# The first scan layer's near part: the product of B with dt·u moved from VectorE to GpSimd, B fetched by DMA

## The chip, the cores and the metric

The kernel runs on one core of a Trainium2 chip. Its time is the device time of one execution in microseconds (us). A core has five engines that work side by side, each through its own queue in order: PE (TensorE, matrix products into PSUM, with a second track PEld for loading weights), DVE (VectorE), ACT (ScalarE), POOL (GpSimd) and SP (SyncE, which here issues almost all DMAs). They wait for each other through semaphores. SBUF is the working memory of 128 partitions; PSUM is the small accumulation memory that TensorE writes.

## The reference

Two layers, each `x = x + layer(groupnorm(x))` on a 64 x 64 image with 96 channels. A layer projects to 192 channels and a gate, applies a depthwise 3 x 3 convolution and silu, runs a selective scan in four directions with 16 states per channel, normalises, gates and projects back. The part that the change touches is the scan of the first layer:

```python
def _ssm_scan(u, x_proj_w, dt_proj_w, dt_proj_b, A_log, D_skip):
    x_dbl = u @ x_proj_w
    dt = x_dbl[..., :DT_RANK]
    B_mat = x_dbl[..., DT_RANK:DT_RANK + D_STATE]
    C_mat = x_dbl[..., DT_RANK + D_STATE:]
    dt = jax.nn.softplus(dt @ dt_proj_w + dt_proj_b)
    A = -jnp.exp(A_log)
    log_dA = jnp.einsum('bld,dn->bldn', dt, A)
    dB_u = jnp.einsum('bld,bln->bldn', dt, B_mat) * u[..., None]
    decay = jnp.exp(jnp.cumsum(log_dA, axis=1))
    h = decay * jnp.cumsum(dB_u / (decay + 1e-12), axis=1)
    y = jnp.einsum('bldn,bln->bld', h, C_mat)
    return y + u * D_skip
...
y1 = scan(s1)
y2 = scan(s1[:, ::-1])[:, ::-1]
y3 = scan(s3)
y4 = scan(s3[:, ::-1])[:, ::-1]
```

`s1` is the image by rows, `s3` by columns. Because of the 1e-12, a state's contribution is damped by decay / (decay + 1e-12), so that it is gone some way into the sequence.

## The kernel before

The layers run one after the other (the code's `l` is 0 for the first). Each has a head (projection, convolution, gate), its scans and a tail (normalisation, gate, projection). The second layer's scans take most of the time, from about 260 to 1440 us, and are not touched.

**The near part.** For the first layer, `near_scans` computes only the first 192 tokens (`NEAR`) of each of the four directions, and of most states less: `kinds` has three entries (n tokens, first and last pair of states): (192, 0, 1), (64, 1, 2) and (32, 2, 8). At the end a flag says whether all that was left out is truly gone; a branch (`tc.If`, line 1729) then skips `far_scans`, and all engines load the flag, branch and meet behind it. The 128 partitions of a tile are two states times 64 channels; T counts three blocks of 64 channels.

**Its parts, in order.** `nu` (three PSUM tiles, one for each T) gathers the tokens of the four directions by matrix products, copied to `nus`; `npj` projects them; the result, with the rows of dt, B and C, is copied to `nxd`. C's rows are stored to DRAM (`nC`) and fetched back, each row spread over 64 partitions (`ncb`, six DMAs). B is spread over partitions on TensorE instead: 18 products `nB<-nxd,picked` into a four-bank PSUM tile, with `picked` a table of ones and zeros that GpSimd writes once. `decays` computes the rates `am`. Softplus gives `nv` on ACT and DVE. `steps_of(T)` makes dt and dt·u (`ndt`, `ndu`) and copies each across the halves by DMA, `sums_of(T)` does so for the running sum of dt (`nS`).

**The units.** There are six: (T0, long), (T0, short), (T1, long), (T1, short), (T2, short), (T2, long), where long is the 192-token kind (768 elements a partition) and short the other two together (256 + 768). Unit j needs, by name: `operands(j)` (ACT: `nna` = exp(rate x dt); GpSimd: a memset of its first columns), `weights_of(j)` (ACT: `nnwt`, a tanh of the sums), and then `scan(j)`, all on DVE but the last: the product `nb<-nB,ndu` (one instruction for a long unit, two for a short one), the product with the weight `nb<-nnwt,nb` (scalar_tensor_tensor, STT below), the scan `nnh<-nna,nb`, and the product with C, `nnhc<-nnh,ncb`, on GpSimd (on DVE for the last unit). `nb` lies in PSUM, so DVE makes it there. `add(j)` sums over states on TensorE into `ny`, whose one PSUM buffer serves one T after the other; `sum_up(T)` adds that to `y` on DVE. The tiles `nna`, `nnwt`, `nnh` and `nnhc` have two buffers each.

**The order.** Engines with `Ordered` around them (line 271, so most instructions here show as L271) keep the order in which the program issues them; what is issued without it (`nc.vector`, `nc.sync`) is placed by the scheduler. In the middle, `look_ahead` issues the second layer's weights, some thirty small DMAs, on SP. GpSimd also scales the six halves of `y` by D (`later`, `y<-u,ds`) early in the near part. Behind the branch, the tail begins with loads of `szt` and `xT` on SP.

Of the kernel before, what the change touches and what calls it, by code (L numbers as in the profile page):

```python
# [21 lines left out]
NS = 16  # L22
# [22 lines left out]
def two_ss2d_layers(  # L45
# [231 lines left out]
    def near_scans(weights, later):  # L277
# [5 lines left out]
        with ExitStack() as sc:  # L283
# [5 lines left out]
            def parts(t):  # L289

                return t.rearrange("p (d w) -> p d w", w=NEAR)
# [8 lines left out]
            top = once.tile([128, len(kinds), 3, 4], F32, name="top")  # L300
            most = once.tile([128, len(kinds) + 1, 3], F32, name="most")
            flag = once.tile([1, 1], mybir.dt.int32, name="flag")
            picked = once.tile([32, NP, 128], F32, name="picked")
            nc.gpsimd.tensor_copy(
                picked.rearrange("p m (h w) -> p m h w", h=2),
                i3[0:32, 0:NS].rearrange("p (m h) -> p m h", h=2)
                .unsqueeze(3)
                .to_broadcast([32, NP, 2, 64]),
            )
            for start in later:  # L310
                start()


            us = once.tile([128, 3, 2, 2 * NEAR], F32, name="nus")
            k = NEAR // HW
            pj = pps.tile([128, 2, 512], F32, tag="m", name="npj")[0:NC, :, 0 : 2 * NEAR]
            for T in range(3):
                ps = pps.tile(
                    [128, 4 if T == 2 else 2, 512], F32, tag="yBB"[T], name=f"nu{T}"
                )[:, 0:2]  # L320
                pe.matmul(
                    ps[:, 0, 0:NEAR], wide[0], u[T][:, 0:NEAR], start=True, stop=True
                )
# [15 lines left out]
                for q, copy in enumerate((act.copy, dve.tensor_copy)):  # L339
                    copy(us[:, T, q], ps[:, q, 0 : 2 * NEAR])  # L340
            for T in range(3):
                for q in range(2):
                    pe.matmul(
                        pj[:, q], xw[HALF[q], 0, T, :], us[HALF[q], T, q],
                        start=(T == 0), stop=(T == 2),
                    )
# [3 lines left out]
            dve.tensor_copy(xq[:, 1], pj[:, 1])  # L350


            C = []
            for w, m0, m1 in kinds:
                rows = dram.tile([NS, 4 * w], F32, name=f"nC{w}")
                sp.dma_start(
                    out=rows.rearrange("n (d w) -> n d w", w=w),
                    in_=parts(xd[NC - NS : NC])[:, :, 0:w],
                )
                C.append(rows)  # L360


            pd = []
            for T in range(3):
# [60 lines left out]
            def reach():  # L425
                for i, (n, m0, m1) in enumerate(kinds):
                    dve.tensor_mul(
                        top[:, i],
                        S.rearrange("p t q (d w) -> p t (q d) w", w=NEAR)[:, :, :, n - 1],
                        most[:, i, :].unsqueeze(2).to_broadcast([128, 3, 4]),  # L430
                    )
                dve.reduce_max(
                    most[:, len(kinds), 0:1], top.rearrange("p i a b -> p (i a b)"), axis=AX.X
                )

                pe.transpose(Bf[0:1, at : at + 128], most[:, len(kinds), 0:1], ident)

            def reached():
                ps = Bf[0:1, at : at + 128]
                dve.reduce_max(most[0:1, len(kinds), 1:2], ps, axis=AX.X)  # L440
                dve.tensor_scalar(flag, most[0:1, len(kinds), 1:2], GONE, None, ALU.is_le)


            Bp = pps.tile([128, 4, 512], F32, tag="B", name="nB")
            Bf = Bp.rearrange("p a b -> p (a b)")
            B, cb, at = [], [], 0
            for n, m0, m1 in kinds:
                B.append([])
                t = once.tile([128, m1 - m0, 4 * n], F32, name=f"ncb{n}")
                for m in range(m0, m1):  # L450
                    dst = Bf[:, at : at + 4 * n]
                    if n == NEAR:
                        for s in (slice(0, 512), slice(512, WN)):
                            pe.matmul(
                                dst[:, s], picked[:, m, :], xd[0:32, s], start=True, stop=True
                            )
                    else:
                        pe.matmul(
                            dst.rearrange("p (d w) -> p d w", w=n), picked[:, m, :],
                            parts(xd[0:32])[:, :, 0:n], start=True, stop=True,  # L460
                        )
                    at += 4 * n
                for h, half in enumerate(HALF):
                    rows = C[len(cb)][2 * m0 + h : 2 * m1 : 2]
                    sp.dma_start(out=t[half], in_=rows.unsqueeze(0).to_broadcast(t[half].shape))
                B[-1] = Bf[:, at - 4 * n * (m1 - m0) : at]
                cb.append(t.rearrange("p n w -> p (n w)"))


            units = [(T, ks) for T in range(3) for ks in ((0,), (1, 2))]  # L470
# [39 lines left out]
                        AF.Tanh, bias=lneps, scale=am[:, 1, 0, T, m : m + 1],  # L510
                    )

            def scan(j):
                T, ks = units[j]
                a, wt, h, hc = live[j]

                b = pps.tile([128, 2, 512], F32, tag="m", name=f"nb{j}")
                b = b.rearrange("p a w -> p (a w)")
                o = 0
                for i in ks:  # L520
                    n, m0, m1 = kinds[i]
                    k = m1 - m0
                    dve.tensor_mul(
                        b[:, o : o + 4 * n * k].rearrange("p (n d w) -> p n d w", n=k, w=n),
                        B[i].rearrange("p (n d w) -> p n d w", n=k, w=n),
                        four(du, T)[:, :, 0:n].unsqueeze(1).to_broadcast([128, k, 4, n]),
                    )
                    o += 4 * n * k
                b = b[:, 0:o]
                dve.scalar_tensor_tensor(b, wt, 1.0, b, ALU.add, ALU.mult)  # L530
                dve.tensor_tensor_scan(h, a, b, 0.0, ALU.mult, ALU.add)
                o = 0
                for i in ks:
# [46 lines left out]
                    dve.tensor_add(to, of, to)  # L580

            steps_of(0)
            steps_of(1)
            sums_of(0)
            steps_of(2)
            operands(0)
# [6 lines left out]
            for j in range(len(units)):  # L593
                if j > 1:
                    weights_of(j)
                if 0 < j < len(units) - 1:
                    operands(j + 1)
                scan(j)
                if j == 1:
                    reach()  # L600
                if j == 2:
# [1219 lines left out]
```

## Time and profile before

| | us |
|---|---|
| median of 4 runs (1469.22 to 1479.03) | 1474.74 |
| the profiled execution | 1472.07 |
| its span, first to last instruction | 1470.3 |
| near part, first `nu` product to the meeting behind the branch | 73.50 to 148.81 |
| the six scans of units on DVE, first start to last end | 107.16 to 140.17 |
| DVE, nine products `nb<-nB,ndu` in all | 7.1 |
| PE, 18 products `nB<-nxd,picked` | 86.75 to 93.09 |
| POOL, six `y<-u,ds` | 75.92 to 92.88 |

The profile's times count from the start of the span. The timeline lists instructions of each engine in order, equal neighbours merged: start, duration, engine, line, operation, output <- inputs, partitions x elements, count, and in brackets how long the engine had been idle and what ended that. SPq is SP's queue: a row there is a DMA being issued, about 0.6 us each, not its transfer. Over the whole span DVE is busy 91%, POOL 82%, ACT 83%; these are averages over both layers, and say little of the near part.

### The profile page before, as it was taken

What the parts mean: (1) busy time and instruction counts of PE and PEld (TensorE: products, weight loads), DVE (VectorE), ACT (ScalarE), POOL (GpSimd) and SP (SyncE); (2) the same over time, 40 slices, a digit from 0 to 9 for tenths busy, and PEclk for the clock granted to TensorE, in tenths of its full rate; (3) what the DMA queues carried; (4) which work ended last, traced back from release to release, by engine and by line L of the source; (5) the groups of instructions that cost most, each with busy time, mean ns of one, the idle gap of its engine ahead of it and who ended that gap; (6) DMA issues with size and microseconds to landing.
All of it is one profiled execution on the core that took longest, in us unless ns stands there. A gap on an engine that the chain in (4) does not pass through costs nothing.

```text
span 1470.3 us, 17235 instructions
## 1 busy us (share of the span) xinstructions
PE 1209.5 (82%) x5011; PEld 469.6 (32%) x5011; DVE 1338.4 (91%) x925; ACT 1218.2 (83%) x2506; POOL 1212.6 (82%) x667
## 2 busy tenths in 40 slices
PE   5845869788888898988888889888879888887897
PEld 2233323233333332333333333333333233322333
DVE  5967677789999999999999999999998999999996
ACT  5764438699898989999999999999897989897874
POOL 2752039588989898989898989898989898989894
PEclk7965979599999899999999989999998999999999
DMA  3231622626262626262626262626262626262634
GB/s 108 82 96 23 148 54 89 131 58 145 58 145 60 143 60 143 60 144 60 144 59 144 60 145 59 150 61 147 61 143 55 148 62 141 72 144 67 136 104 111
DMA packets 85556, 147.70 MB, mean 100 GB/s; under 512 B 33436, under 2 KB 36700, under 8 KB 85356
## 3 DMA queue, kind: packets, MB, share of 16 engines
q1 hardware_dynamic: 83772, 143.96, 41.3%
q0 software_dynamic: 576, 1.57, 0.5%
q8 instruction: 41, 0.67, 0.2%
q10 hardware_dynamic: 1104, 0.98, 0.2%
q14 instruction: 63, 0.52, 0.1%
HBM read 80.85 MB, written 12.13 MB: 63 GB/s over the span
## 4 chain that ended last, share of the span: by engine, by line
DVE 26%; issue 20%; PE 13%; ACT 13%; POOL 8%; DMA 6%; SPq 3%; DVEq 0%; POOLq 0%; ACTq 0%
DVE h L751 17%; DVE b L751 7%; POOL hc L751 5%; ACT a L751 4%; DMA cb<-C 4%; SPq L751 3%; PE pj L751 3%; ACT bT L751 3%; PE ys L751 3%; PE b L751 2%; DMA xT<-xs 1%; POOL sp L751 1%; POOL ln L751 1%; DMA dt<-sp 1%; PE cp L271 1%
## 5 line engine op out<-in xcount | busy, mean ns | idle before, releaser
L751 POOL TENSOR_TENSOR hc<-h,cb 128x1024 f32<-128x1024 f32 x384 | 902.6, 2370 | 94.7 <-DVE h L751 37.9
L751 DVE TENSOR_TENSOR_SCAN h<-a,carry,b 128x1024 f32<-128x1024 f32 x288 | 664.9, 2338 | 24.0 <-PE b L751 2.8
L751 ACT ACTIVATE a<-dt,am 128x1024 f32<-128x1024 f32 x384 | 439.2, 1144 | 57.6 <-DVE h L751 54.5
L751 PE MATMUL ys<-hc,fold 128*64 128x512 f32 x1536 | 430.6, 640 | 0.0
L751 ACT ACTIVATE bT<-duT,BT 128x192 f32<-128x192 f32 x1012 | 387.9, 447 | 2.9 <-PE b L751 0.8
L751 PE MATMUL b<-ident,bT 128*128 128x128 f32 x1536 | 223.2, 288 | 30.4 <-DVE h L751 19.5
L751 DVE TENSOR_TENSOR b<-b,du 128x1024 f32<-128x1024 f32 x192 | 232.0, 1208 | 8.4 <-PE b L751 8.4
L751 DVE TENSOR_TENSOR_SCAN h<-a,b 128x1024 f32<-128x1024 f32 x96 | 216.4, 2278 | 13.2 <-PE b L751 3.4
L751 PEld LDWEIGHTS b<-ident,bT 128*128 128x128 f32 x1536 | 176.6, 146 | 154.7 <-DVE h L751 92.2
L751 PE MATMUL b<-B,selh 96*128 96x512 bf16 x384 | 117.2, 387 | 125.3 <-DVE h L751 125.1
L751 PEld LDWEIGHTS ys<-hc,fold 128*64 128x64 f32 x1536 | 77.9, 138 | 140.4 <-issue 104.5
L751 PEld LDWEIGHTS <-selh 96*128 96x128 bf16 x384 | 25.7, 98 | 254.1 <-DVE h L751 203.0
L751 PE MATMUL pj<-u,xw 64*124 64x512 f32 x192 | 96.5, 649 | 1.9 <-DVE w L751 1.2
L271 POOL TENSOR_TENSOR tap<-tap,tap 128x512 f32<-128x512 f32 x48 | 61.0, 1275 | 44.3 <-ACT tap L271 42.0
L271 DVE SCALAR_TENSOR_TENSOR acc<-pad,v,acc 128x1052 f32<-128x1052 f32 (+1 forms) x64 | 75.2, 1181 | 2.1
L751 ACT CAST B<-pj 96x512 bf16<-96x512 f32 (+2 forms) x96 | 55.0, 576 | 6.1 <-PE pj L751 6.1
L751 PE MATMUL ys<-y,ident 128*128 128x512 f32 (+1 forms) x120 | 58.9, 592 | 0.0
L751 POOL TENSOR_TENSOR ln<-ln,w 128x512 f32<-128x512 f32 x45 | 57.7, 1283 | 0.0
L751 POOL TENSOR_TENSOR sp<-sp,ln 128x512 f32<-128x512 f32 x45 | 57.6, 1280 | 0.2
L751 POOL TENSOR_TENSOR su<-sp,u 128x512 f32<-128x512 f32 x45 | 57.4, 1276 | 0.0
L751 PE MATMUL pd<-xd,dwb 29*64 29x512 f32 x192 | 54.5, 636 | 0.0
L751 PEld LDWEIGHTS pj<-u,xw 64*124 64x124 f32 x192 | 34.4, 194 | 60.8 <-issue 47.3
(188 smaller groups left out, 1188.0 us busy)
## 6 DMA issues: line engine op xcount, KB each, us to landing
cb<-C SPq DMA_DIRECT2D x256, 256.0 KB
dt<-sp SPq DMA_DIRECT2D x192, 128.0 KB
du<-su SPq DMA_DIRECT2D x180, 128.0 KB
szd<-sz SPq DMA_DIRECT2D x24, 256.0 KB
szt<-szd SPq DMA_DIRECT2D x24, 256.0 KB
xT<-xs SPq DMA_DIRECT2D x8, 384.0 KB
xs<-xT SPq DMA_DIRECT2D x1, 1536.0 KB
xs<-xT SPq DMA_DIRECT2D x8, 192.0 KB
```

The lines of the kernel that those rows point to most:

```text
L271: return lambda *args, **more: tc.keep_in_program_order(op(*args, **more))
L751: return lambda *args, **more: tc.keep_in_program_order(op(*args, **more))
```

## The change

- `picked` and the 18 products that spread B over partitions are gone, and with them the four-bank PSUM tile. The PSUM tiles are dealt out anew: `nu` gets one two-bank buffer for each T (tags y, m, B), `npj` and the test of the flag one of their own (tag j).
- B's rows go the way of C's: two stores to DRAM, six fetches, each row to 64 partitions, now to SBUF. Of B and C alike only the rows of 192 and of 32 tokens are stored; those of 64 are fetched as a cut of the 192. In all, SP issues 16 such DMAs for 9.
- The fetches of C's second and third kind (four DMAs) come after `steps_of(1)`; before, all six stood ahead of `steps_of(0)`.
- The product of B with dt·u is `inputs(j)`, on GpSimd, into an SBUF tile with two buffers; for units 0 and 1 right after `steps_of(0)`, for unit j + 2 after `scan(j)`.
- `scan(j)` begins with the STT, which reads both factors from SBUF and writes PSUM, in two buffers used by turns.

```diff
-            picked = once.tile([32, NP, 128], F32, name="picked")
-            nc.gpsimd.tensor_copy(
...
-            pj = pps.tile([128, 2, 512], F32, tag="m", name="npj")[0:NC, :, 0 : 2 * NEAR]
+            
             for T in range(3):
-                ps = pps.tile(
-                    [128, 4 if T == 2 else 2, 512], F32, tag="yBB"[T], name=f"nu{T}"
-                )[:, 0:2]
+                ps = pps.tile([128, 2, 512], F32, tag="ymB"[T], name=f"nu{T}")
...
+            pj = pps.tile([128, 2, 512], F32, tag="j", name="npj")[0:NC, :, 0 : 2 * NEAR]
...
+            def stored(what, first):
+
+                kept = {}
+                for w in (NEAR, kinds[-1][0]):
+                    rows = dram.tile([NS, 4 * w], F32, name=f"n{what}{w}")
+                    rows = kept[w] = rows.rearrange("n (d w) -> n d w", w=w)
+                    sp.dma_start(out=rows, in_=parts(xd[first : first + NS])[:, :, 0:w])
+                return kept
+
+            def fetched(what, kept, i):
+
+                n, m0, m1 = kinds[i]
+                t = once.tile([128, m1 - m0, 4, n], F32, name=f"n{what}b{n}")
+                for h, half in enumerate(HALF):
+                    if n in kept:
+                        to, of = t[half], kept[n][2 * m0 + h : 2 * m1 : 2]
+                    else:
+                        to, of = t[half, 0], kept[NEAR][2 * m0 + h, :, 0:n]
+                    sp.dma_start(out=to, in_=of.unsqueeze(0).to_broadcast(to.shape))
+                return t.rearrange("p n d w -> p (n d w)")
+
+            rows = stored("B", 0)
+            B = [fetched("B", rows, i) for i in range(len(kinds))]
+            rows = stored("C", NC - NS)
+            cb = [fetched("C", rows, 0)]
...
-            def scan(j):
+            def inputs(j):
                 T, ks = units[j]
-                a, wt, h, hc = live[j]
-
-                b = pps.tile([128, 2, 512], F32, tag="m", name=f"nb{j}")
-                b = b.rearrange("p a w -> p (a w)")
+                b = live["b", j] = nb.tile([128, 1024], F32, tag="nb", name=f"nb{j}")
                 o = 0
                 for i in ks:
                     n, m0, m1 = kinds[i]
                     k = m1 - m0
-                    dve.tensor_mul(
+                    pool.tensor_mul(
                         b[:, o : o + 4 * n * k].rearrange("p (n d w) -> p n d w", n=k, w=n),
                         B[i].rearrange("p (n d w) -> p n d w", n=k, w=n),
                         four(du, T)[:, :, 0:n].unsqueeze(1).to_broadcast([128, k, 4, n]),
                     )
                     o += 4 * n * k
-                b = b[:, 0:o]
-                dve.scalar_tensor_tensor(b, wt, 1.0, b, ALU.add, ALU.mult)
+
+            def scan(j):
+                T, ks = units[j]
+                a, wt, h, hc = live[j]
+                w = a.shape[-1]
+                b = pps.tile([128, 2, 512], F32, tag="mB"[j % 2], name=f"nbw{j}")
+                b = b.rearrange("p a w -> p (a w)")[:, 0:w]
+                dve.scalar_tensor_tensor(b, wt, 1.0, live.pop(("b", j))[:, 0:w], ALU.add, ALU.mult)
                 dve.tensor_tensor_scan(h, a, b, 0.0, ALU.mult, ALU.add)
...
             steps_of(0)
+            inputs(0)
+            inputs(1)
             steps_of(1)
+            cb += [fetched("C", rows, i) for i in range(1, len(kinds))]
             sums_of(0)
...
                 scan(j)
+                if j + 2 < len(units):
+                    inputs(j + 2)
```

More of the change, by code (lines that the diff above doesn't have):

```diff
@@ L302, in near_scans @@
             flag = once.tile([1, 1], mybir.dt.int32, name="flag")
-            picked = once.tile([32, NP, 128], F32, name="picked")
-            nc.gpsimd.tensor_copy(
[L305 to L309, printed above, removed]
             for start in later:
@@ L350, in near_scans @@
             dve.tensor_copy(xq[:, 1], pj[:, 1])
[L353 to L360, printed above, removed]
+            def stored(what, first):
[19 more added lines that the diff above has]
+            cb = [fetched("C", rows, 0)]
             pd = []
@@ L434, in reach @@
                 )
-                pe.transpose(Bf[0:1, at : at + 128], most[:, len(kinds), 0:1], ident)
+                live["most"] = pps.tile([128, 2, 512], F32, tag="j", name="nmost")[0:1, 0, 0:128]
+                pe.transpose(live["most"], most[:, len(kinds), 0:1], ident)
             def reached():
-                ps = Bf[0:1, at : at + 128]
-                dve.reduce_max(most[0:1, len(kinds), 1:2], ps, axis=AX.X)
+                dve.reduce_max(most[0:1, len(kinds), 1:2], live.pop("most"), axis=AX.X)
                 dve.tensor_scalar(flag, most[0:1, len(kinds), 1:2], GONE, None, ALU.is_le)
[L444 to L467, printed above, removed]
             units = [(T, ks) for T in range(3) for ks in ((0,), (1, 2))]
```

## The prediction, made before the changed kernel ran

> **What bounds the kernel now.** I read the windows of the near part first, then its timeline, then the chain of waits behind the branch. The windows (busy us of each engine and instructions in brackets):
>
> ```profile
> core 0: us, PE busy (x) PEld busy (x) DVE busy (x) ACT busy (x) POOL busy (x), PEclk, DMA share, GB/s
> 73.00:97.00 24.00, 18.27 (x82) 12.71 (x78) 13.68 (x20) 13.18 (x24) 19.13 (x10) 0.78 0.27 78
> 97.00:125.97 28.97, 7.44 (x19) 4.38 (x19) 23.15 (x30) 24.21 (x58) 6.88 (x12) 0.50 0.39 80
> 125.97:148.81 22.84, 11.92 (x38) 8.90 (x38) 15.10 (x26) 1.85 (x2) 5.03 (x5) 0.65 0.12 16
> ```
>
> In the units' stretch (second row) DVE and ACT are equally full and POOL is idle three quarters of the time. So DVE's products are worth something only where ACT isn't the one waited for. The timeline says where:
>
> ```profile
> 102.18 1.19 SPq L271 DMA_DIRECT2D nS<-nS  x2
> 105.04 1.03 ACT L271 ACTIVATE nnwt<-nS,lneps,am 128x768 f32<-128x768 f32 x1 [2.37 <-DMA nS<-nS]
> 106.10 0.96 DVE L271 SCALAR_TENSOR_TENSOR nb<-nnwt,nb 128x768 f32<-128x768 f32 x1 [2.77 <-ACT nnwt L271]
> ...
> 109.19 2.89 ACT L271 ACTIVATE nnwt<-nS,lneps,am 128x256 f32<-128x256 f32 x7
> 112.02 0.17 DVE L237 TENSOR_REDUCE ds<-v 128x3 f32<-128x12 f32 x1 [1.64 <-DMA v<-in_vec_dram]
> 112.13 1.23 DVE L271 SCALAR_TENSOR_TENSOR nb<-nnwt,nb 128x1024 f32<-128x1024 f32 x1
> ...
> 127.86 1.43 DVE L271 TENSOR_TENSOR nb<-nB,ndu 128x256 f32<-128x256 f32 x2
> 127.98 6.27 PE L271 MATMUL ny<-nnhc,fold 128*128 128x512 f32 x18 [6.66 <-DVE y L271]
> 134.29 1.96 DVE L271 TENSOR_TENSOR y<-ny,y 64x192 f32<-64x192 f32 x6 [1.27 <-PE ny L271]
> ```
>
> The first weight waits for a DMA that SP issued at 102.18, and SP has issued without a gap since 97.06. Unit 1's STT waits for its tanhs (109.19 + 2.89 = 112.08). Unit 4's product lies beside the 6.27 us in which PE sums T1, for which DVE waits anyway. Behind the units:
>
> ```profile
> L1729 SPq EVENT_SEMAPHORE  x8: 17/17/17, 145.8 to 148.1; - x8
> L1729 DVEq EVENT_SEMAPHORE  x1: 21/21/21, 148.8 to 148.8; - x1
> ...
> 150.62 6.52 DMA xT<-xs
> 157.14 0.02 issue
> 157.16 10.24 DMA xT<-xs
> ```
>
> SP's last act at the meeting is at 148.1, DVE's at 148.81. From there the chain goes over SP's issues into transfers. So whoever comes last to the meeting moves the rest one for one, and SP has only 0.7 us to spare.
>
> **The change, part by part.**
>
> *Gathering.* PE's only wait here was 1.16 us, the third `nu` for the copies of the second; each has its own buffer now. But the first `nu` now takes PSUM's first banks, held by the gate until its silu ends at 73.67 + 0.60 = 74.27, where before it began at 73.50. Gain 1.16 - 0.77 = 0.4 us (ends: a loss of 0.8, a gain of 1.2).
>
> *`picked` and the 18 products.* PE works on them from 86.75 to 93.09 and then idles to 111.33: nothing. On POOL the copy of 1.03 us goes, so the six scalings of `y` start 1.0 earlier. That matters through two odd rows:
>
> ```profile
> 84.34 2.93 DVE L247 TENSOR_SCALAR am<-am 128x24 f32<-128x24 f32 x1
> 87.31 2.79 DVE L248 TENSOR_SCALAR am<-am 128x24 f32<-128x24 f32 x1
> ...
> 84.40 5.66 POOL L271 TENSOR_SCALAR y<-u,ds 128x1024 f32<-128x1024 f32 x2
> ```
>
> 24 elements should take 0.2 us (the second layer's smallest is 0.189 for 48). Both end where a scaling ends (84.40 + 2.83 = 87.23, + 2.83 = 90.06). DVE thus waits for POOL here, and T0's first `nv`, at 90.34, behind both. One us earlier on POOL puts these ends at 86.3 and 89.1: gain 0.95. If the first `am` got in ahead of the end at 83.5, `nv` would wait only for ACT (88.21 less the gathering's gain), a gain of 2.5 to 3.3; its start is due at 84.34 - 0.4 = 83.9, so I take 0.95.
>
> *SP ahead of the units.* B's stores and fetches cost 7 more issues of 0.63 (`ncb`: 3.78 for six), 4.4 us, and C must now be stored behind B's fetches, a second wait for a store. SP idles from 92.19 to 97.06, 4.87 us. With stores at 84.95, first fetch 2.39 later as before (85.35 to 87.74), six fetches to 91.1, two stores to 92.2, again 2.39 from the first store, two fetches: 94.8. dt is due at 96.1, so: nothing. If three loads of `ab`, which now fill gaps there, add their 1.9 us, dt is 0.6 late; if the landing takes a us more each time, 2.6.
>
> *C's later fetches.* Four issues, 2.5 us, stand ahead of `nS` on a full SP: `nS` of T0 and everything SP issues behind it moves by -0.95 + 2.5 = +1.55. Their 512 KB take some 2 us at the 252 GB/s of the fetches before, and are issued over 2.5, so `nS` finds little queue (0 to +2). Behind SP wait: the first tanh on ACT, then all of ACT's row up to `nnwt` of unit 1, DVE's first two units, and SP's own arrival.
>
> *Nine products off DVE* (three of 0.96, three of about 1.42: 7.1 us). Units 0 and 1: nothing, DVE waits there for ACT (2.77 us; 112.08). Units 2 and 3: from the end of unit 1's scan, 115.75, to that of unit 3, 125.97, are 10.22 us. Now ACT decides: `nna` 2.26 and `nnwt` 2.89 behind that scan, STT 1.23, scan 2.29, gaps: 8.75. Gain 1.5. Unit 4: nothing (hidden by PE). Unit 5: 0.97 and its gap, 1.05, on the way between `sum_up(1)` and the end. Together 2.5 of 7.1.
>
> *The same products on POOL.* No row has them; `nnhc` of the same sizes takes 1.81 (768) and 2.51 (256 + 768), 2.36 ns an element. This is the lower end. The upper is POOL's `bT<-duT,BT`, 0.755 for 192 elements in pieces of 64, 3.9 ns, 4.0 us for a short unit. I take 2.36, the nearer row. Unit 3's then ends at 2.51 (`nnhc` of unit 1) + 2.51 = 5.02 behind unit 1's scan, as late as `nnwt` (5.1): nothing. At 4.0 us: +1.4. The memset that the scan needs queues behind it, but 0.17 us, under the STT. Units 0 and 1 run while everyone waits for `nS`.
>
> *STT from SBUF.* 0.96 and 1.23 were with PSUM on one side. An STT from SBUF twice, `nw<-nt,nw`, took 0.56 with POOL idle and 0.75 once with POOL working: between +0 and +34%, that is up to 0.4 on each of four that are on the path (units 0, 1, 3, 5), 0 to 1.4. I take 0.4. [...]
>
> **Sum.** DVE's arrival: 148.81 + 1.55 - 1.5 - 1.05 + 0.4 = 148.2. SP's: 148.1 + 1.55 = 149.65. SP is last; the meeting moves from 148.81 to about 149.7, +0.8 us, and the tail behind it with it. DVE's relief is real and goes into waiting for SP. The profiled execution becomes 1472.07 + 0.8 = 1472.9; the median stands 2.67 above it, so 1475.5 on the scale of the median. Own bounds: -3.5 (early `am`, `ab` loads moved into the gaps, which takes up to 3.1 off SP's end, DVE last) to +5 (late landings 2.6, slower products or STTs). Runs spread by -5.5 and +4.3 around their median, which I add in part: 1467 to 1483. 0.5% is 7.4 us, about what a measurement of this kernel can tell from no change.
>
> **The rivals.**
>
> *DVE's time counts in full.* All 7.1 us come off, with 1.2 at the gathering and 2.5 at `am`: 10.8 less, 1464. For it: DVE is busy 23.15 of 28.97 us. Against: its rows for units 0, 1 and 4 show waits that the products fill. It would need ACT and SP to be early too. Chance 0.13 for anything faster by over 0.5%.
>
> *SP's queue takes DVE's place.* If none of the added issues (4.4) or the second landing (2.4) fits in the idle stretch, and C's transfers hold up `nS` by 2, the first tanh is 8.8 later, less 0.95, and the meeting +7.2 (SP's 0.7 taken off): 1482 to 1483. For it: SP is full from 97.06 to 142.2 and leads the chain behind the meeting. Against: 4.87 us of idle time and the small transfers. It decides from the point where dt's DMA is issued after 97.06. Chance 0.21 for slower by over 0.5%; a lesser form, 2 to 5 us, lies in the forecast's range.
>
> *POOL is the bound.* At 3.9 ns an element it costs 1.4 at unit 3 and little behind it, since POOL's queue then ends under PE's 6.27 us: 1477. Only at three times the price of `nnhc` would it pass 0.5%; no row comes near. It is within the 0.66 that I give to no change.
>
> So: 0.13 faster, 0.66 within 0.5%, 0.21 slower; the range leaves 2 in 10 outside, more of it above than below.
>
> **What would show it.** Right: `nS` of T0 issued at 103 to 104.5; the first tanh still waiting for it; unit 3's STT released by ACT or POOL and not by DVE's own row; DVE idle behind PE for over 2 us at `sum_up(1)`; SP last at the meeting, near 149.7. Wrong: POOL products over 3 us for 768 elements, STTs over 1.4, the `ds` reduction (which waits for a load behind `nS` on SP) ahead of unit 0's STT on DVE, or a meeting outside 146 to 153. A change of over 7 us with a meeting inside those would mean that something outside the near part moved.

## The result, and the profile after

The changed kernel takes 1479.82 us in the median of 42 runs (1470.89 to 1486.12), the kernel before 1473.33 us (68 runs, 1468.45 to 1483.59). Taken side by side on the same chip the ratio is 1.0035, with a 95% interval of 1.0023 to 1.0047: slower by 0.35%, some 5.2 us, and so within the 0.5% that the forecast called no change. The profiled execution of the changed kernel took 1480.99 us, its span is 1479.2 us, 8.9 more than before.

In these two profiles the near part itself is not slower: from the first `nu` product to POOL's first work behind the meeting it takes 74.25 us (74.42 to 148.67), against 75.57 (73.50 to 149.07). The first experiment shows how far that holds. These are the windows of the changed kernel's near part, with the columns shown before: gathering and steps, the stretch of the units up to the end of the fourth scan, and the rest up to the meeting.

```profile
core 0: us, PE busy (x) PEld busy (x) DVE busy (x) ACT busy (x) POOL busy (x), PEclk, DMA share, GB/s
74.42:97.00 22.58, 11.04 (x60) 8.11 (x60) 12.17 (x24) 15.06 (x28) 17.55 (x9) 0.77 0.29 74
97.00:129.18 32.18, 7.44 (x19) 4.39 (x19) 16.68 (x20) 20.59 (x51) 17.45 (x18) 0.50 0.47 99
129.18:148.67 19.49, 8.68 (x39) 6.20 (x40) 13.63 (x24) 2.39 (x4) 9.48 (x9) 0.85 0.10 16
```

In the units' stretch DVE's work fell from 23.15 to 16.68 us and POOL's rose from 6.88 to 17.45, as planned; yet the stretch grew from 28.97 to 32.18, since what it waits for in its first part is a DMA. The timeline of the changed kernel shows that wait:

```profile
96.34 1.18 SPq L271 DMA_DIRECT2D ndt<-ndt  x2
...
101.43 2.61 SPq L271 DMA_DIRECT2D nCb<-nC  x4
104.15 1.21 SPq L271 DMA_DIRECT2D nS<-nS  x2
...
108.29 1.03 ACT L271 ACTIVATE nnwt<-nS,lneps,am 128x768 f32<-128x768 f32 x1 [6.04 <-DMA nS<-nS]
...
109.42 0.97 DVE L271 SCALAR_TENSOR_TENSOR nbw<-nnwt,nb 128x768 f32<-128x768 f32 x1 [10.06 <-ACT nnwt L271]
```

C's four late fetches stand between dt's DMAs and `nS`: `nS` goes out at 104.15 (before: 102.18), and it lands 4.1 us later instead of 2.9, so the first tanh starts at 108.29 (105.04). Further on, in the units, the same timeline shows the new pair of engines at work on SBUF:

```profile
114.48 1.81 POOL L271 TENSOR_TENSOR nb<-nBb,ndu 128x768 f32<-128x768 f32 x1
...
115.37 2.01 DVE L271 SCALAR_TENSOR_TENSOR nbw<-nnwt,nb 128x1024 f32<-128x1024 f32 x1 [0.72 <-ACT nnwt L271]
...
125.56 1.23 DVE L271 SCALAR_TENSOR_TENSOR nbw<-nnwt,nb 128x1024 f32<-128x1024 f32 x1 [1.94 <-POOL nna L271]
125.57 2.87 POOL L271 TENSOR_TENSOR nnhc<-nnh,nCb 128x768 f32<-128x768 f32 x1
...
131.19 4.88 PE L271 MATMUL ny<-nnhc,fold 128*128 128x512 f32 x18 [5.14 <-DVE y L271]
...
136.11 1.97 DVE L271 TENSOR_TENSOR y<-ny,y 64x192 f32<-64x192 f32 x6 [0.96 <-PE ny L271]
```

The POOL product in the first row takes the predicted 1.81 us. Five of the six STTs overlap a POOL product in this profile, and each time one of the two grows, or both: the STT at 115.37 takes 2.01 us for 1.23, and beside the STT at 125.56 `nnhc` takes 2.87 for 1.81. In the last two rows PE's 18 products take 4.88 us for 6.27 before, and DVE waits only 0.96 for them.

At the meeting, these are its semaphores in the changed kernel (kind, count, min/median/max in ns, first and last start):

```profile
L1719 SPq EVENT_SEMAPHORE  x8: 17/17/17, 145.3 to 145.8; - x8
...
L1719 DVEq EVENT_SEMAPHORE  x1: 21/21/21, 148.4 to 148.4; - x1
```

DVE comes last, at 148.4 (before 148.8), and SP is done 2.6 us ahead of it. So between these two profiles the meeting moved by -0.4 while the execution got 8.9 us longer. The difference lies behind it, in code that the change doesn't touch. The second layer's scans begin at 274.4 us (before 274.5) and run in lockstep with those of before until 367. These windows of before, then of the changed kernel, show how they part:

```profile
core 0: us, PE busy (x) PEld busy (x) DVE busy (x) ACT busy (x) POOL busy (x), PEclk, DMA share, GB/s
...
366.00:374.00 8.00, 7.32 (x32) 2.44 (x30) 7.87 (x5) 6.90 (x15) 8.00 (x5) 1.00 0.00 1
...
393.00:404.00 11.00, 10.83 (x43) 4.21 (x42) 10.73 (x6) 9.81 (x22) 11.00 (x7) 1.00 0.35 95
```

```profile
core 0: us, PE busy (x) PEld busy (x) DVE busy (x) ACT busy (x) POOL busy (x), PEclk, DMA share, GB/s
...
366.00:374.00 8.00, 8.00 (x23) 2.76 (x22) 6.14 (x5) 7.00 (x14) 8.00 (x6) 0.57 0.00 1
...
393.00:404.00 11.00, 11.00 (x27) 3.85 (x24) 7.55 (x4) 6.12 (x15) 11.00 (x7) 0.53 0.38 97
```

The reader is to look at PEclk. In both stretches PE is granted full clock before (1.00) and little more than half after (0.57, 0.53); PE is then busy all the time and DVE loses 1.73 and 3.18 us of work. The second layer makes 384 scans, one in each of its units. From unit 20 on I took them in fours and set each four against the quickest that any of my profiles shows at that place. The sum, called excess below, is 11.1 us in the profile before and 20.9 in the one after. More than half of it lies in a few fours and comes mostly in two sizes: 1.6 to 2.2 us where the unit's number divided by 24 leaves 4 (28, 76 and so on), 4.3 us where it leaves 12 (36, 84). These fours make up 6.2 us of the excess before and 16.1 after, the whole difference. The two stretches above are those of units 28 and 36.

Two theories stand from here. FRONT: the loss arises before the second layer's scans. LATER: it arises in them. For LATER there are again two: PHASE (the granted clock, which in both profiles changes only at instants 3.413 us or a multiple of it apart, changes at other places of the same instructions) and STATIC (the changed program makes them slower in every execution). For the near part: SPQ (SP's queue sets the first tanh) and PORT (STTs with both inputs in SBUF and POOL's products slow each other down).

### The profile page after: what moved, and what is told of

It is laid out like the page before. It is cut to its first block, busy times and chain, and to the rows that moved or that the text cites. A ratio compares the mean times of both kernels' runs of the same rounds, so it can differ in the third digit from the quotient of the medians.

```text
span 1479.2 us, 17206 instructions
## 1 busy us (share of the span) xinstructions
PE 1205.2 (81%) x4993; PEld 463.5 (31%) x4993; DVE 1329.6 (90%) x916; ACT 1216.7 (82%) x2506; POOL 1226.3 (83%) x675
## 4 chain that ended last, share of the span: by engine, by line
DVE 27%; issue 20%; PE 15%; ACT 9%; POOL 9%; DMA 6%; SPq 3%; DVEq 0%; POOLq 0%; ACTq 0%
DVE h L741 18%; DVE b L741 8%; POOL hc L741 7%; PE pj L741 4%; PE ys L741 4%; DMA cb<-C 4%; ACT a L741 3%; PE b L741 3%; SPq L741 2%; ACT bT L741 2%; DMA dt<-sp 1%; DMA szt<-szd 1%; POOL sp L741 1%; PE cp L271 1%; POOL ln L741 1%
```

## The experiments

### Where the loss lies: both kernels cut behind the second layer's head

Both kernels end ahead of the second layer's scans; the edit is the same.

```diff
+            rows = out.rearrange("l c -> (l c)").rearrange("(p f) -> p f", p=128)
+            nc.sync.dma_start(out=rows[:, 0 : L // 2], in_=u[0])
+            nc.sync.dma_start(out=rows[:, L // 2 :], in_=u[2][:, 0 : L // 4])
+            return
```

> The kernel before, cut off after the second layer's head: the second layer's scans and last tail are left out, and part of u is written as output. It gives the time of everything up to about 262 us of the trace without the second layer's scans, in several runs. Expected 265 to 275 us. It is the reference for the next one.

> The changed kernel with the same cut. Theory FRONT (the near part itself is slower in most executions, and the one profiled was a lucky one because PE's clock came up early in it): its median lies 3 to 6 us above that of the cut kernel before. Theory LATER (the profile is typical: both reach the second layer's scans at the same time, -0.1 us, and the difference arises in the second layer's scans through PE's granted clock): its median lies within 1 us of the cut kernel before.

Before, cut: 255.40 us (254.98 to 256.59, 5 runs; 265 to 275 were expected). After, cut: 257.78 us (257.66 to 257.96, 5 runs). The difference of 2.4 us lies between the theories: about half of the 5.2 us is lost in front, the rest in the scans behind. The timelines of the two cut kernels, before first, give the front part's start and end:

```profile
74.22 4.20 PE L271 MATMUL nu<-u,wide 128*128 128x192 f32 x24
...
148.92 3.51 POOL L1742 MEMSET xT<- 1x4096 f32 x1 [12.65 <-PE m L1494]
```

```profile
75.40 6.16 PE L271 MATMUL nu<-u,wide 128*128 128x192 f32 x36 [0.75 <-ACT sz L271]
...
149.91 3.51 POOL L1732 MEMSET xT<- 1x4096 f32 x1 [10.23 <-DVEq L1723]
```

`nu` starts 1.2 us later, 0.75 of it the wait for the gate's silu. By POOL's memset the near part then takes 74.51 us for 74.70, and is no slower. But POOL's memset is not what the tail waits for. These rows are of the kernel before with a delay in the second layer (its near part is unchanged; it comes again below), then of the changed kernel:

```profile
147.23 3.75 PE L1498 MATMUL m<-y,pos 128*128 128x512 f32 x4 [4.49 <-DVEq L1733]
...
149.78 3.51 POOL L1742 MEMSET xT<- 1x4096 f32 x1 [12.78 <-SPq L1733]
149.85 0.36 SPq L1489 DMA_DIRECT2D szt<-szd  x1
```

```profile
148.53 1.19 PE L1484 MATMUL m<-y,pos 128*128 128x512 f32 x1 [4.58 <-DVEq L1719]
148.56 1.00 SPq L1475 DMA_DIRECT2D szt<-szd  x2
...
148.67 3.51 POOL L1728 MEMSET xT<- 1x4096 f32 x1 [10.01 <-DVEq L1719]
```

In the first, DVE releases PE, and PE starts the tail 2.6 us ahead of SP and POOL, since SP is last at the meeting; in the second DVE is last and all start together. Yet from PE's first product there to the last activation of the second layer's head it is 99.4 to 100.0 us in every profile of the record, whether SP comes first or up to 2.6 us after DVE. So the tail follows PE, which DVE's arrival releases, and SP's lateness costs nothing there. Measured from `nu` to PE's start, the near part takes 72.4 to 73.2 us in four of the five profiles of before (the cut one among them) and 73.9 to 74.6 in the five of the changed kernel, with the cut one and those with a delay. The first profile of before is the exception, with 75.4: PE had about half the clock while it summed there (more on this below). In the four others SP is last at the meeting, in all five of the changed kernel DVE.

So the near part is some 1.4 us slower where it counts, and with `nu`'s delay that is the front part of the loss. (`nu` itself varies: it starts at 73.5 to 75.4 us in the five profiles of before, at 74.4 to 76.1 in the five of the changed kernel.) PE starts the tail at 149.77 us in the changed kernel's cut profile and at 146.85 in that of before, and the last activation of the second layer's head comes 2.7 us later (249.36 for 246.64). Two stretches say what the near part lost and won. From `nu` to the first STT it is 32.6 us in all five of before and 34.8 to 35.5 in the five of the changed kernel, 2.4 more. From there to PE's start it is 39.8 to 40.6 us in the four of before and 39.0 to 39.4, about 1.1 less: that is all that came of DVE's 7.1 us.

### How much one profile says: both kernels again, unchanged

> The changed kernel as it is, to have a second profile of it beside more times. LATER: the second layer's scans start within 0.5 us of the first profile's 274.4, and whatever differs behind that follows the places where PE is granted half its clock. FRONT: they start 3 us or more later than 274.5.

> The kernel before against itself: ratio 1.000 within its interval, and a second profile of it. LATER with a clock grid that runs free of the program: its half-clock windows lie at another offset to the program than in the first profile (0.96 us into the 3.41 us grid), and its scans differ from the first profile's by some us with the windows. If the grid is tied to the program, the offset is 0.96 again.

The changed kernel: 1475.38 us (12 runs, 1469.37 to 1484.52), ratio 1.003 (1.0005 to 1.0055). The kernel before: 1468.95 us (12 runs, 1464.9 to 1476.43) beside 1472.38 in 23 other runs of the same kernel, ratio 0.9981 (0.9959 to 1.0003). The loss repeats, though one kernel differs from itself by 0.2% here. The near part repeats too (`am` 0.93 and 0.18 us, the same late `nS`), but the second layer's scans begin at 275.5, which the expectation had within 0.5 of 274.4: `nu` was a us later in that execution. The excess was 15.7 us after and 9.5 before, at other places than the first time. The instants at which the granted clock changes lie on a grid of 3.413 us in every profile, but its offset against the program's start was 0.96 and 0.73 us in the two of before, and 1.21 and 2.48 in the two of the changed kernel. So one program meets the grid in different ways, and no single profile stands for it.

### SP's queue: C's four late fetches later still

```diff
             steps_of(1)
-            cb += [fetched("C", rows, i) for i in range(1, len(kinds))]
             sums_of(0)
...
             sums_of(2)
+            cb += [fetched("C", rows, i) for i in range(1, len(kinds))]
```

> The changed kernel with one step moved: the four fetches of C's second and third kind are issued behind the DMAs of the sums instead of ahead of them. Theory SPQ (these four set the first tanh): from dt's first DMA to the first tanh it takes 8.0 us as in the kernel before instead of 11.9, and the end of the sixth unit's scan comes 3 to 4 us earlier behind the first nu product (67 us in the changed kernel: 74.4 to 141.35). Rival PORT (the units are slow because of GpSimd, whatever their start): the first tanh comes earlier, but the sixth scan ends less than 1.5 us earlier.

One execution: 1473.33 us. The timeline of this kernel:

```profile
102.47 1.20 SPq L271 DMA_DIRECT2D nS<-nS  x2
...
105.34 1.03 ACT L271 ACTIVATE nnwt<-nS,lneps,am 128x768 f32<-128x768 f32 x1 [2.16 <-DMA nS<-nS]
...
108.87 2.61 SPq L271 DMA_DIRECT2D nCb<-nC  x4
```

From dt's DMA (97.34 here, 96.34 in the changed kernel) to the first tanh it is 8.0 us instead of 11.9, and `nS` lands 2.9 us behind its issue again. The sixth scan ends 63.3 us behind `nu` instead of 66.9, and PE starts the tail 70.55 us behind `nu` instead of 74.11. (POOL and SP start at 71.81, for SP is last at the meeting here.) SPQ is shown: these four issues with their transfers cost 3.6 us in the near part, and without them it is shorter than in any profile of before. All STTs but the last stayed as long (0.97, 2.01, 1.27, 1.23, 1.68, 0.97), so the long ones have another cause.

### PORT: the tanh weights into PSUM

The weights `nnwt` are written to PSUM, so that no STT reads SBUF twice. To make room `nbw` has one buffer, and the flag's test takes a free piece of `ny`.

```diff
-                live["most"] = pps.tile([128, 2, 512], F32, tag="j", name="nmost")[0:1, 0, 0:128]
+                live["most"] = live["y"][0:1, 1, 256:384]
...
+                wt = pps.tile([128, 2, 512], F32, tag="Bj"[j % 2], name=f"nwt{j}")
+                wt = wt.rearrange("p a w -> p (a w)")[:, 0:long]
...
-                b = pps.tile([128, 2, 512], F32, tag="mB"[j % 2], name=f"nbw{j}")
+                b = pps.tile([128, 2, 512], F32, tag="m", name=f"nbw{j}")
```

> The changed kernel with the tanh weights written to PSUM, so that the scalar_tensor_tensor of a unit reads one factor from SBUF and one from PSUM; the test of the flag uses a free piece of another PSUM tile. Theory PORT (two SBUF inputs collide with GpSimd): the six take 0.96 and 1.23 us again, as in the kernel before, instead of 0.97, 2.01, 1.27, 1.23, 1.69, 1.38, GpSimd's products with C 1.8 instead of up to 2.9, and the six scans take 1 to 2 us less from the first's start to the last's end (30.9). Rival WRITE (it is the transfers or GpSimd's writes, not the reads): the durations stay above 1.2 and 1.6.

One execution: 1479.29 us. The group of STTs in this kernel (min/median/max ns, first to last start), and then in the changed kernel:

```profile
L271 DVE SCALAR_TENSOR_TENSOR nbw<-nwt,nb x6: 956/1100/1233, 110.9 to 140.5; 128x768 f32<-128x768 f32 x3, 128x1024 f32<-128x1024 f32 x3
```

```profile
L271 DVE SCALAR_TENSOR_TENSOR nbw<-nnwt,nb x6: 968/1328/2014, 109.4 to 138.1; 128x768 f32<-128x768 f32 x3, 128x1024 f32<-128x1024 f32 x3
```

With one input in PSUM no STT passes 1.233 us, for 2.014, and POOL's longest `nnhc` fell from 2.871 to 1.814 us, though both engines do the same work side by side. The kernel before, with one input in PSUM too, has no longer ones either (1.229 and 1.815 us). So PORT is shown, in the sense that the second input in SBUF makes the long ones; what the two engines share there no run shows. But from the first scan's start to the last one's end it is 31.3 us, for 30.9 in the changed kernel, where 1 to 2 us less were expected. Two rows of this kernel's timeline say what may have taken the gain:

```profile
114.09 3.52 ACT L271 ACTIVATE nwt<-nS,lneps,am 128x256 f32<-128x256 f32 x7
...
126.87 0.28 DVE L271 TENSOR_REDUCE most<-ny 1x1 f32<-1x128 f32 x1 [2.43 <-PE ny L271]
```

Seven small tanhs into PSUM take 3.52 us for 2.89 into SBUF, on the engine that a short unit waits for, and the flag's test now waits 2.43 us for PE's sums. PE's 18 products also took 5.56 us in this execution, for 4.88. No run separates the three.

### The clock's grid: delays at the start of the second layer's scans

If PHASE held and the delay shifted the scans on the grid, a delay of a few us should make the kernel before lose what the changed one loses, and the reverse. DVE gets reductions behind the second layer's unit 16, whose result nothing uses. In the changed kernel, one of 0.39 us:

```diff
+                if j == 16:
+                    dve.reduce_max(wait, selh[:, 0:2].rearrange("p q h c -> p (q h c)"), axis=AX.X)
```

> The changed kernel with one extra VectorE reduction of 256 elements (about 0.4 us) in the second layer's scans, behind unit 16. Theory PHASE (how many half-clock windows PE gets in the second layer hangs on where its scans fall on the clock's 3.41 us grid; the changed kernel starts them at 0.13 and -0.05 on it, the kernel before at 0.48 and 0.36): it lands at about 0.45 and becomes faster by 3 to 8 us, ratio 0.998 to 1.001 to the kernel before. Rival STATIC (something else in the second layer is slower): it stays at 1.003 or above.

1472.19 us (12 runs), ratio 1.0008 (0.9987 to 1.003). The number is near the expected one, but not for its reason: scans up to unit 20 took 71.4 us as without the reduction, so that it was absorbed, and the profile shows losses at units 28 and 36 as the changed kernel's first did. It is one more sample of the changed kernel, and not a test.

In both kernels, 3.2 us:

```diff
+                    dve.reduce_max(wait, selh[:, 0:16].rearrange("p q h c -> p (q h c)"), axis=AX.X)
+                    dve.reduce_max(wait, selh[:, 0:6].rearrange("p q h c -> p (q h c)"), axis=AX.X)
```

> The kernel before with two extra VectorE reductions (2048 and 768 elements, about 3.1 us together) at the same place. PHASE: it lands at 0.1 on the grid, where the changed kernel is, and loses 6 to 11 us: ratio 1.004 to 1.0075. STATIC: it loses its own 3.1 us at most: 1.002.

> The changed kernel with the two extra VectorE reductions (3.2 us; in the kernel before they delayed the scans by 1.3 us, the rest fell into a wait) in the second layer's scans behind unit 16. Theory PHASE, in its sharper form: the first group's loss (units 28 to 40, 1.84 + 4.3 us) came in all three executions that reached unit 20 at 3.23 to 3.37 us on the clock's grid (first profile, a_d04, a_clate), and in none of the five that reached it at 0.10 to 0.25 or 1.42 to 1.48. Moved by 1.3 us it lands at 1.1 to 1.4: no loss in units 28 to 40, and the ratio to the kernel before is 1.000 to 1.003 in spite of the added 1.3 us. STATIC: 1.0044 or more.

Up to unit 20 the scans took 72.7 us with the delay in the kernel before and 71.8 in the changed one, for 71.4 to 71.5 in the first profile of each: of the 3.2 us only 1.3 and 0.4 took effect. Before with it: 1473.73 us, ratio 1.0021 (1.0004 to 1.0038), which misses PHASE's 1.004 to 1.0075. After with it: 1471.91 us, ratio 1.0012 (0.9994 to 1.0031); no loss in units 28 to 40, as expected, but losses at 76 and 84, and it reached unit 20 at 2.43 us on the grid where 1.1 to 1.4 were expected. STATIC's 1.0044 lies outside the interval; but the interval overlaps that of the first measurement (1.0023 to 1.0047), and the changed kernel with the 0.39 us that were absorbed came to 1.0008 without any shift. So this doesn't rule STATIC out.

And in the kernel before a longer one, meant to put it where the changed kernel's first profile was (here 16, then 15, then 2 in the first index):

```diff
+                    dve.reduce_max(wait, selh[:, 0:16].rearrange("p q h c -> p (q h c)"), axis=AX.X)
+                    dve.reduce_max(wait, selh[:, 0:15].rearrange("p q h c -> p (q h c)"), axis=AX.X)
+                    dve.reduce_max(wait, selh[:, 0:2].rearrange("p q h c -> p (q h c)"), axis=AX.X)
```

> The kernel before with three such reductions (2048, 1920 and 256 elements, 4.8 us, of which 1.8 should fall into the wait again). PHASE: it moves by 3.0 us, reaches unit 20 at 3.1 to 3.3 us on the grid where the kernel before did so at 0.10 to 0.25, and now shows the first group's loss (1.8 at units 28 to 31 and 4.3 at 36 to 39); ratio 1.004 to 1.007. STATIC: no such loss, its own 3.0 us: 1.002.

1472.96 us, ratio 1.0016 (1.0000 to 1.0033): missed again, it is about the 2.9 us that the delay itself cost. It landed at 2.98 us of the grid and showed only the small loss. What the profiles give together (position on the grid at unit 20; units whose four lost 4.3 us; excess from unit 20 on, which the added reductions lie ahead of):

| profile | position, us | units with 4.3 us | excess, us |
|---|---|---|---|
| before | 0.25 | 276 | 11.1 |
| before, again | 0.10 | 156 | 9.5 |
| before, 3.2 us | 1.43 | 228 | 12.7 |
| before, 4.8 us | 2.98 | none | 6.2 |
| after | 3.31 | 36, 84 | 20.9 |
| after, again | 1.48 | 156 | 15.7 |
| after, 0.39 us | 3.23 | 36, 252 | 16.4 |
| after, 3.2 us | 2.43 | 84 | 11.0 |
| C late | 3.37 | 36, 276 | 17.9 |
| tanh weights in PSUM | 1.42 | 156 | 14.6 |
| last version (below) | 1.46 | 60 | 14.5 |

The loss at unit 36 shows in the three profiles that came in at 3.23 to 3.37 us, and in none of the others; the mean excess is 9.9 us in the four of before and 15.9 in the seven of the changed kernel and its versions, whose instructions here are the same. That is a pattern over eleven executions. No run put a kernel at a place of the grid on purpose, and moving the kernel before by 1.3 and 2.9 us didn't bring the changed kernel's time, so PHASE as the cause of the median's loss stays open. The same runs also show how sure the size of the loss is: for the changed kernel, with and without a reduction that costs it little, the ratios were 1.0035, 1.003, 1.0008 and 1.0012.

### The version that the experiments point to

All six fetches of C behind the sums (the first kind behind `sums_of(1)`, the others behind `sums_of(2)`), and `npj` takes its PSUM ahead of `nu`, so that `nu` doesn't wait for the gate.

```diff
+            pj = pps.tile([128, 2, 512], F32, tag="j", name="npj")[0:NC, :, 0 : 2 * NEAR]
             for T in range(3):
...
-            cb = [fetched("C", rows, 0)]
...
-            cb += [fetched("C", rows, i) for i in range(1, len(kinds))]
             sums_of(0)
...
             sums_of(1)
+            cb = [fetched("C", rows, 0)]
...
             sums_of(2)
+            cb += [fetched("C", rows, i) for i in range(1, len(kinds))]
```

> The changed kernel with all six fetches of C behind the sums' DMAs (the first two behind those of T1, the others behind those of T2), and npj's PSUM buffer taken first, so that the first nu product no longer waits for the gate's silu. Theory SPQ: dt's first DMA no longer waits for C's store and goes out 2.4 us earlier, nu begins 0.8 us earlier, and from the first nu product to the meeting it takes 69 to 70.5 us (75.1 in the kernel before, 74.2 in the changed one, 71.8 in a_clate). In the whole time this shows only as far as PE's clock lets it: ratio 0.995 to 1.000. Rival: what the front saves is taken back in the tail or in the second layer, ratio 1.001 or more.

> The same, cut off after the second layer's head like b_front (255.4 us) and a_front (257.78 us); the second layer's scans and last tail are left out. SPQ: 250 to 253.5 us. If the tail takes it back: 254.5 or more.

Whole: 1470.41 us (12 runs, 1462.16 to 1480.8), ratio 0.9993 (0.9968 to 1.0018): the same as before. Cut like the two above: 252.4 us (250.04 to 255.28, 6 runs), 3.0 less than before cut and 5.4 less than the changed kernel cut, but on another chip than those two. Its profiled execution, the slowest of the six, reached the end of the second layer's head at 247.0 us, for 249.4 in the changed kernel and 246.6 before. So the trace shows a saving in front against the changed kernel; against the kernel before it isn't shown, in front or in the whole time, and the whole profile's excess was 14.5 us. From `nu` to PE's start the near part took 72.25 us, 1.7 to 2.4 less than the changed kernel, and 72.38 to POOL's, where 69 to 70.5 were expected. Its timeline says why:

```profile
110.32 2.67 DVE L271 SCALAR_TENSOR_TENSOR nbw<-nnwt,nb 128x1024 f32<-128x1024 f32 x1 [3.00 <-ACT nnwt L271]
...
111.87 2.78 POOL L271 TENSOR_TENSOR nb<-nBb,ndu 128x768 f32<-128x768 f32 x1
...
121.17 2.91 DVE L271 SCALAR_TENSOR_TENSOR nbw<-nnwt,nb 128x1024 f32<-128x1024 f32 x1 [1.84 <-POOL nna L271]
```

With SP out of the way, the STTs lie beside a POOL product for longer (8.9 us in all, for 5.7 in the changed kernel) and take up to 2.91 us for 1.23; the six together take 10.7 us for 8.6. The longer STTs take part of what the queue gave, and C late, with 70.55 us, has the shortest near part of all.

## Why the forecast's number held, and where its steps failed

The forecast was no change, 0.8 us more; the kernel became 5.2 us slower, inside the 0.5% and inside the range. That is in part luck. The fetches' cost and the small worth of DVE's relief were read rightly, but the forecast held the wrong engine's arrival for the one that moves the tail, it built on one execution whose PE clock was low at the sums, several terms were mis-sized, and half of the 5.2 us came from behind the near part, where it put nothing. Of its own signs, one of being wrong came: STTs over 1.4 us (2.01 and 1.69). Two of being right did not: DVE idle behind PE for over 2 us at `sum_up(1)` (0.96), and SP last at the meeting.

*Gathering* (0.4 us gained). Right: `nu` waits 0.74 us for the gate's silu, the later wait is gone, `nxd` comes at 82.84 instead of 83.35, a gain of 0.5.

*`am` ends with a scaling* (0.95, or 2.5 to 3.3 "if the first `am` got in ahead of the end"). The reading failed. These rows of the changed kernel:

```profile
80.80 11.29 POOL L271 TENSOR_SCALAR y<-u,ds 128x1024 f32<-128x1024 f32 x4
...
83.83 0.93 DVE L247 TENSOR_SCALAR am<-am 128x24 f32<-128x24 f32 x1
...
84.79 0.18 DVE L248 TENSOR_SCALAR am<-am 128x24 f32<-128x24 f32 x1
```

The four scalings follow each other every 2.82 us, the second from 83.62 to 86.45; both `am` run and end inside it, in 1.11 us together. T0's `nv` came 3.1 us earlier. In all profiles of before the first `am` starts 0.03 to 0.06 us ahead of a scaling, and the two take 2.8 to 2.9 us each (the second, in the first profile, from 0.09 behind a scaling's start); in the changed kernel the first starts 0.2 behind a scaling's start, and they take 0.93 and 0.18. In the last version two that started 0.6 ahead of a scaling and 0.08 behind its start took 0.66 and 1.05. Which rule grants it I can't say.

*SP ahead of the units* (nothing). The sum put C's fetch so that dt would not wait. The earlier `nv` made dt ready about 94, but SP was not free for its first DMA until 96.34 (the sum had SP free at 94.8). The gain of 3.1 at `am` shrank to 0.7 here. The changed kernel's rows say what SP did:

```profile
91.81 1.20 SPq L271 DMA_DIRECT2D nC<-nxd  x2
93.05 0.61 SPq L218 DMA_DIRECT2D ab<-in_alb_dram  x1
93.71 0.60 SPq L222 DMA_DIRECT2D ab<-in_alb_dram  x1
94.36 0.60 SPq L218 DMA_DIRECT2D ab<-in_alb_dram  x1
95.11 1.13 SPq L271 DMA_DIRECT2D nCb<-nC  x2
```

The step priced a wait for the store's landing at 2.39 us. But SP does not stand still between store and fetch: the 3.3 us here are two stores and three loads of `ab`, one behind the other, and the 2.39 before were three stores and one load. What a landing takes is in neither. Four more of these loads than before stand ahead of dt; the forecast had priced three such loads as a possible loss and left them out of its sum.

*C's later fetches* (`nS` +1.55, and 0 to 2 for their transfers). Right: +1.97, at 104.15 within the 103 to 104.5 named; from issue to the tanh it took 1.3 us more, and the first tanh is 3.25 late. Taking the four away from there gave 3.6 back.

*Nine products off DVE* (units 2 and 3: 1.5; unit 5: 1.05). From unit 1's scan end to unit 3's, 10.2 became 9.4 us: 0.8. Unit 3's STT was released by POOL, as foreseen, but POOL's `nnhc` took 3.21 us for 2.51, beside an STT. At unit 5, 0.65, since its STT took 1.38 us. The rival that counts DVE's 7.1 us in full fell: DVE's busy time went, its waits stayed.

*The products on POOL* (2.36 ns an element). Right: 1.80 to 1.81 us for 768 elements and 2.48 for 256 and 768 where nothing disturbs them; the upper end of 3.9 ns didn't occur in the changed kernel.

*STT from SBUF* (0.4, at most 1.4). Mis-sized: the six took 8.6 us for 6.6, 2.0 more, and POOL's `nnhc` grew by up to 1.06 beside them. With two SBUF inputs the STT took 2.01 us for 1.23 beside POOL's product; with one input in PSUM none took over 1.233. The bound came from one row of a smaller instruction (0.75 for 0.56) beside a scaling on POOL, which reads one tile; POOL's products read two.

*SP last at the meeting* (149.65), and whoever is last moves the tail. Both failed. Seven of the eight loads of `ab`, three before, now stand ahead of dt's DMAs, so SP arrived at 145.8 and DVE was last. And the tail follows PE, which DVE releases: in four profiles of before SP came 1.3 to 2.6 us behind that, at no cost to the tail. The forecast had named the loads among its bounds ("`ab` loads moved into the gaps, which takes up to 3.1 off SP's end, DVE last") and not taken it.

*PE's 6.27 us at `sum_up(1)`*, behind which unit 4's product lay and DVE was to wait over 2 us. That was one execution's clock: 0.52 while the 18 products ran, for 0.68 in the changed kernel, and 0.50 for 1.00 while the last six ran. The same 18 products took 5.39, 4.83 and 5.36 us in three other profiles of before, and 4.88 and 5.05 in two of the changed kernel; the last six took 2.93 in the first profile and 1.56 in all of these. From the first STT to the end DVE made up 3.5 us in the changed kernel: -0.7 up to unit 1's scan end (the long STT), 0.8 and 0.65 as above, and 2.8 from PE's clock at `sum_up(1)` and `sum_up(2)` (1.38 each). The other profiles of before had already what PE's clock gave here. Against them the units gave only 1.1 us and the late `nS` took 2.4, so that DVE released the tail some 1.4 us later behind `nu`, where the forecast had it 0.6 earlier.

*Outside the near part* (nothing). The forecast's last sentence gave the sign: a change of over 7 us with a meeting inside the bounds means that something else moved. The profiled execution did just that. In the medians of the cut kernels it is 2.4 us up to the second layer's scans: 1.2 at `nu` in their profiles, of which the gathering's term had 0.77, and 1.7 in the near part up to PE's start. The rest lies behind that. Of the rest the first two profiles show that the scans run in lockstep but for a few half-clock windows of PE. Not settled is whether the changed kernel meets bad places of the grid more often in general, or loses there in every execution; the delays that were to decide it missed their places.

## What to carry to other kernels

A product moved to an idle engine is worth only what the waits behind it let through: follow the queue that feeds the next wait (here SP's, with each added fetch and its transfer) before the busy shares. STTs with two SBUF inputs and GpSimd products beside them took up to 2.4 times as long here, on either engine (2.91 us for 1.23 on DVE, 1.70 for 0.72 on GpSimd, in the last version), so an instruction that loses its PSUM input is better priced as overlapping. And for changes under 0.5%, look at more than one profile of the same kernel before a PE duration goes into a sum: the granted clock alone moved two terms here by 1.4 us each, and changed which engine came last at the meeting. The engine that comes last is also not always the one that what follows waits for.

## What the runs showed of the hardware

- In these profiles the granted clock was full (1.0) or half (0.5) and changed only on a grid of 3.413 us: all 57 changes in the first profile of each kernel lie on one. The grid's offset against the program's start differs between executions (0.96 and 0.73 us in the two unchanged profiles of before, 1.21 and 2.48 in the two of the changed kernel), though four of the fourteen profiles have the same within 0.01 us, 0.96. The second layer's loop runs nearly in step with this grid: 24 of its scans take 72.1 us in the median of the first profile of before (72.4 in the changed kernel's), and 21 windows are 71.7. In the profile of before half-clock windows begin at 513.0, 584.6, 656.3, 728.0 and 799.7 us, each time 24 scans later (units 75, 99, 123, 147, 171).
- DVE's 24-element `am` took 2.93 us beside the scalings on POOL where it began 0.06 us ahead of one, and 0.93 and then 0.18 where it began 0.2 behind a start. What decides it the case doesn't show.
- A GpSimd product with one operand broadcast and runs of only 32 elements cost no more an element than `nnhc`, whose operands are plain (1.80 us for 768 elements, 2.48 for 256 and 768, against 1.81 and 2.50).
- ACT's seven tanhs of 128 or 256 elements took 3.52 us into PSUM and 2.89 into SBUF, though one of 128 takes 0.46 us into PSUM and 0.48 into SBUF.
